# Sums taken on VectorE in halves before two chains of TensorE products, in the edge sort of a graph layer

## The chip, the cores and the metric

The kernel runs on one core of a Trainium2 chip. Its time is the device time of one execution in microseconds (us). TensorE is called PE in the profile, VectorE is DVE, ScalarE is ACT, GpSimd is POOL, and SyncE is SP.

## The reference

There are 8192 nodes with 512 features, and 131072 edges (src, dst, weight), sorted by dst.

```python
h   = layernorm(x) @ gnn_weight.T
msg = edge_weight[:, None] * h[dst]
x   = x + segment_sum(msg, src, 8192)      # added up by src
x   = x + ffn(layernorm(x))                # seven layers of width 160 on two positions of a row,
                                           # their inputs and the output of 32 columns are one-hot nibbles
```

The edges are sorted by dst, but the sum is over src. So the kernel must first bring the edges into the order of their src block (64 blocks of 128 nodes), and then gather rows of h by dst.

## The kernel before

**Projection** (`project`, lines 176 to 245): a loop over the 64 blocks of 128 rows. VectorE takes the statistics of a pair of blocks, ScalarE scales it, TensorE turns a block (L213, four transposes) and multiplies it with the weights (L238), ScalarE evicts, and SP writes h_rows to memory. The statistics and scaled rows are issued four blocks ahead.

**The sort** (`order`, L537) is done in two parts, of 7 and 9 chunks. Each part goes through its chunks (`chunk`, L328) and then a squeeze (`squeeze`, L410), which closes the gaps in the placed cells. A chunk holds 64 edges in each of 128 partitions, as 8 columns c of 8 groups g. It does this:

- VectorE builds `hot`, the one-hot of the src block of each edge (128 x 8 x 64 x 8, bf16; L334).
- TensorE adds up, over the partitions above and all columns, how many edges of each block there are: `p_base`, eight accumulating products with the matrix `above` (L342). ScalarE copies it to `cum[:, 0]` (L344).
- VectorE forms running sums over the columns in `cum` (L347) and masks them with `hot` (L351). Each edge has one block, so in a masked column only one of 64 values counts.
- TensorE sums these: eight products with the identity add eighths of the 64 blocks into `p_rank` (L357), and VectorE reduces the last eight (L361).
- VectorE turns a rank into a slot (`at`, L376) and two value tiles (`put`, L384); ScalarE copies `hot` to f32 as `blocks` (L375); TensorE places the edges with many small products, `p_c` (L402), in four bursts, each of which the trace shows as 64 matrix instructions.

The tiles `hot`, `cum` and the others of a chunk have one buffer each; `put` and `blocks` have two.

**The order of work.** PE, DVE, ACT and SP issue in the order of the program text, which a planner with generators writes. `chunk` and `squeeze` yield a pair (tiles, blocks): how many gather tiles, or projection blocks, are to be issued before the next step. A zero means that the next step follows at once.

The first part runs beside the projection, and only `blocks` counts: a chunk takes six blocks, and base and rank are issued two blocks apart, with `fine` off, so that an operation is not cut. Once the first part ends, up to BEGUN steps of the second part are issued in the projection's last blocks, and then the steps up to number BEGUN + 16:

```python
while first is None and begun < BEGUN and due <= b + 1:
    due += next(second)[1]
    begun += 1
...
for n in range(BEGUN + 16):
    if n >= begun:
        next(second)
```

The rest of the second part runs beside the first gathers (`begin`, L874), with `fine` on, so that an operation is cut into pieces. There `tiles` counts, multiplied with PACE (the first value for chunks, the second for the squeeze):

```python
while t >= due:
    due += next(second, (NB * FT,))[0]
```

**Gathers.** GpSimd fetches rows of h by index (`rows_for`, L570, one indirect DMA per tile of 128 edges, four tiles per buffer, six buffers). For a tile, VectorE builds a weighted one-hot (L583), issued 28 tiles ahead, and TensorE multiplies it with the rows (L870, two instructions per tile in the trace, and one small `p_j` product per buffer, L866). VectorE adds a finished block to x (L880). The first part has 6 tiles per block, 384 in all (`begin`); the second 11, 704 in all (`evenly`, L903), with the network (`ffn`, L693) beside them. The second part's gathers need the second squeeze, which is issued to its end by tile 355.

Of the kernel before, what the change touches and what calls it, by code (L numbers as in the profile page):

```python
# [9 lines left out]
BF16 = mybir.dt.bfloat16  # L10
# [3 lines left out]
OP = mybir.AluOpType  # L14
# [20 lines left out]
def tile_gnn_ffn(  # L35
# [23 lines left out]
    nc = tc.nc  # L59
    P = 128  # L60
    N, D = x.shape
    E = src.shape[0]
    NB = N // P
# [7 lines left out]
    GC, GQ, CAP, SUB = 8, 8, 40, 2  # L71
# [13 lines left out]
    GS = 4  # L85


    SHARE, TURN, WIDTH, PACE = 0.5, 0.6, 640, (1.0, 0.85)
    assert E % P == 0 and D == 512 and NB == 64 and N <= 1 << DSTS and LOW + BITS <= 31
    assert N % (P * U) == 0 and GB * NG == P and all(NB * n % GS == 0 for n in TILES)  # L90

# [173 lines left out]
    above = ec.tile([P, P], BF16, name="above")  # L265
# [57 lines left out]
    def cut(n, size, fine):  # L323

        parts = -(-n // size) if fine else 1
        return [slice(n * i // parts, n * (i + 1) // parts) for i in range(parts)]

    def chunk(ck, ps_c, q, col, fine):  # L328


        hot = ck.tile([P, GC, NB, GQ], BF16, name="hot")
        for cs in cut(GC, 2, fine):
            n = cs.stop - cs.start
            nc.vector.tensor_tensor(  # L334
                hot[:, cs], each.rearrange("p (o b) g -> p o b g", o=1).to_broadcast([P, n, NB, GQ]),
                blk[:, q, cs].rearrange("p c (o g) -> p c o g", o=1).to_broadcast([P, n, NB, GQ]),
                OP.is_equal)
            yield 1, cs.stop // GC

        p_base = ps_c.tile([P, NB, GQ], F32, name="p_base")  # L340
        for c in range(GC):
            nc.tensor.matmul(p_base, above, hot[:, c], start=(c == 0), stop=(c == GC - 1))  # L342
        cum = ck.tile([P, GC, NB, GQ], BF16, name="cum")
        nc.scalar.copy(cum[:, 0], p_base)  # L344
        yield 2, 0
        for c in range(1, GC):
            nc.vector.tensor_tensor(cum[:, c], cum[:, c - 1], hot[:, c - 1], OP.add)  # L347
            if c % 2:
                yield 1, 0
        for cs in cut(GC, 2, fine):  # L350
            nc.vector.tensor_tensor(cum[:, cs], cum[:, cs], hot[:, cs], OP.mult)  # L351
            yield 1, 0
        yield 0, 2
        p_rank = ps_c.tile([P, GC, NB // GC, GQ], F32, name="p_rank")
        nb = NB // GC
        for i in range(GC):
            nc.tensor.matmul(p_rank, eye, cum[:, :, i * nb : (i + 1) * nb, :], start=(i == 0),  # L357
                             stop=(i == GC - 1))
        yield 2, 0
        rank = ck.tile([P, GC, GQ], F32, name="rank")  # L360
        nc.vector.tensor_reduce(rank, p_rank.rearrange("p c b g -> p c g b"), AX.X, OP.add)  # L361
        slot = ck.tile([P, CG, 1], BF16, name="slot")
        nc.vector.tensor_tensor(slot[:, :, 0], rank.rearrange("p c g -> p (c g)"), par, OP.add)
        yield 1, 0
        at = ck.tile([P, CG, 2, HALF], BF16, name="at")
        ready = {}

        def prepare(c0):

            if c0 >= GC:  # L370
                return
            n = SUB * GQ
            cs = slice(c0 * GQ, c0 * GQ + n)
            blocks = ck.tile([P, SUB, GQ, NB], F32, name="blocks", bufs=2)
            nc.scalar.copy(blocks, hot[:, c0 : c0 + SUB].rearrange("p c b g -> p c g b"))  # L375
            nc.vector.tensor_tensor(  # L376
                at[:, cs].rearrange("p n h s -> p n (h s)"),
                lots.rearrange("p (o h) s -> p o (h s)", o=1).to_broadcast([P, n, CAP]),
                slot[:, cs].to_broadcast([P, n, CAP]), OP.is_equal)
            yield 1, 0  # L380
            put = ck.tile([P, n, 2, 2, HALF], F32, name="put", bufs=2)
            for i, val in enumerate((val_a, val_w)):
                v = val[:, q, c0 : c0 + SUB, :].rearrange("p c (g a b) -> p (c g) a b", a=1, b=1)
                nc.vector.tensor_tensor(put[:, :, :, i, :], at[:, cs],  # L384
                                        v.to_broadcast([P, n, 2, HALF]), OP.mult)
                yield 1, 0
            ready[c0] = blocks, put

        yield from prepare(0)
        yield 0, 1  # L390
        yield from prepare(SUB)
        p_c = ps_c.tile([P, GQ, 2, HALF], F32, name="p_c")
        yield 0, 1
        nc.tensor.matmul(p_c.rearrange("p g w s -> p (g w s)"), nil[:, :P], nil, start=True,
                         stop=False)
        for c0 in range(0, GC, SUB):
            blocks, put = ready.pop(c0)
            for k in range(SUB * GQ):
                c, g = divmod(k, GQ)
                last = c0 + SUB == GC and k == SUB * GQ - 1  # L400
                for h in range(2):
                    nc.tensor.matmul(p_c[h * NB : (h + 1) * NB, g], blocks[:, c, g, :], put[:, k, h],  # L402
                                     start=False, stop=last)
            yield from prepare(c0 + 2 * SUB)
            yield 1, c0 // SUB % 2 if c0 + SUB < GC else 0
        for i, cells in enumerate((cells_a, cells_w)):
            nc.scalar.copy(cells[:, col : col + GQ * HALF].rearrange("p (g s) -> p g s", s=HALF),
                           p_c[:, :, i, :])
# [128 lines left out]
    def order(part):  # L537

        qs, col, fine = (range(QA), 0, 0) if part == 0 else (range(QA, NQ), CARRY, 1)
        with tc.tile_pool(name="ck", bufs=1) as ck, \  # L540
                tc.tile_pool(name="ps_c", bufs=1, space=PSUM) as ps_c:
            for q in qs:
                for tiles, blocks in chunk(ck, ps_c, q, col, fine):
                    yield tiles * PACE[0], blocks
                col += GQ * HALF
        with tc.tile_pool(name="sq", bufs=1) as sq, \
                tc.tile_pool(name="ps_q", bufs=2, space=PSUM) as ps_q:
            for tiles, blocks in squeeze(part, sq, ps_q, fine):
                yield tiles * PACE[1], blocks
# [42 lines left out]

    LEAD, BEGUN = 2, 24
    due, early, begun = LEAD, 0, 0
    for b, _ in enumerate(heads):
        while first and due <= b + 1:
# [548 lines left out]
```

## Time and profile before

| | us |
|---|---|
| median of 3 runs (2081.74 to 2099.45) | 2087.55 |
| the profiled execution | 2087.88 |
| its span, first to last instruction | 2086.0 |
| PE busy | 1752.6 (84%) |
| DVE busy | 988.5 (47%) |
| ACT busy | 389.3 (19%) |
| POOL busy | 1113.9 (53%) |
| p_base products, L342, x128 | 31.7 busy |
| p_rank products, L357, x128 | 31.8 busy |
| first indirect gather starts at | 369.7 |
| second squeeze starts at | 836.5 |

The busy time of an engine is the union of its instructions, so that eight products that overlap in the pipeline count once. The mean of one product (393 ns) includes the time to its modelled end; the time from one start to the next is what a product takes from the others. In a line of the timeline the bracket at the end gives the idle time of the engine before the instruction, and what released it. The granted clock of TensorE is given as a share of full speed; its mean over the execution is 0.908.

### The profile page before, as it was taken

What the parts mean: (1) busy time and instruction counts of PE and PEld (TensorE: products, weight loads), DVE (VectorE), ACT (ScalarE), POOL (GpSimd) and SP (SyncE); (2) the same over time, 40 slices, a digit from 0 to 9 for tenths busy, and PEclk for the clock granted to TensorE, in tenths of its full rate; (3) what the DMA queues carried; (4) which work ended last, traced back from release to release, by engine and by line L of the source; (5) the groups of instructions that cost most, each with busy time, mean ns of one, the idle gap of its engine ahead of it and who ended that gap; (6) DMA issues with size and microseconds to landing.
All of it is one profiled execution on the core that took longest, in us unless ns stands there. A gap on an engine that the chain in (4) does not pass through costs nothing.

```text
span 2086.0 us, 24100 instructions
## 1 busy us (share of the span) xinstructions
PE 1752.6 (84%) x9288; PEld 845.7 (41%) x9288; DVE 988.5 (47%) x2520; ACT 389.3 (19%) x521; POOL 1113.9 (53%) x1138
## 2 busy tenths in 40 slices
PE   7999989589889988976877697896978969697977
PEld 4555544344444444322332243342434334243444
DVE  6676787365545554983332334233333334234422
ACT  5565644211201211110000010100101001010111
POOL 4000000466657666787666666666666766666540
PEclk9999999699989998988999899998989979898986
DMA  5233332567667776677876667686676857667651
GB/s 174 82 102 102 102 93 84 150 198 218 209 205 217 220 222 214 191 229 226 259 264 190 174 186 262 181 274 174 191 258 176 275 169 218 217 172 244 198 148 35
DMA packets 140923, 391.37 MB, mean 188 GB/s; under 512 B 20352, under 2 KB 21376, under 8 KB 140800
## 3 DMA queue, kind: packets, MB, share of 16 engines
q0 software_dynamic: 87952, 286.45, 46.0%
q1 hardware_dynamic: 52048, 101.72, 14.4%
q8 instruction: 76, 1.25, 0.2%
q10 hardware_dynamic: 800, 1.57, 0.2%
q14 instruction: 47, 0.39, 0.1%
HBM read 339.33 MB, written 50.33 MB: 187 GB/s over the span
## 4 chain that ended last, share of the span: by engine, by line
PE 65%; issue 10%; DVE 9%; another core or an unknown queue 8%; POOL 6%; DMA 2%; ACT 1%; POOLq 0%; DVEq 0%; ACTq 0%
PE p_g L870 36%; PE p_g L238 8%; PE p_c L402 7%; POOL g L570 6%; PE p_a L666 2%; PE p_a L668 2%; DVE hot L583 2%; PE p_rank L357 1%; PE p_base L342 1%; DMA g<-h_rows,at_dst 1%; PE p_g L213 1%; PE p_j L866 1%; PE p_b L660 1%; DVE ln L706 1%
## 5 line engine op out<-in xcount | busy, mean ns | idle before, releaser
L570 POOL DMA_INDIRECT g<-h_rows,at_dst x1088 | 1091.6, 1003 | 906.7 <-issue 645.2
L870 PE MATMUL p_g<-g,hot 128*128 128x512 f32 x2176 | 1098.9, 640 | 42.1 <-issue 42.0
L870 PEld LDWEIGHTS p_g<-g,hot 128*128 128x128 f32 x2176 | 407.6, 201 | 438.9 <-issue 428.0
L583 DVE TENSOR_SCALAR hot<-lanes,at_row,at_w 128x128 f32<-128x128 f32 x1088 | 325.6, 354 | 235.5 <-remote 143.7
L238 PE MATMUL p_g<-xg,g 128*128 128x512 f32 x512 | 235.8, 604 | 5.1 <-ACT g L215 5.1
L402 PE MATMUL p_c<-put,blocks 128*64 128x40 f32 x4096 | 163.9, 237 | 66.0 <-issue 62.7
L402 PEld LDWEIGHTS p_c<-put,blocks 128*64 128x64 f32 x4096 | 147.6, 146 | 110.0 <-issue 102.4
L375 ACT CAST blocks<-hot 128x1024 f32<-128x1024 bf16 x64 | 131.4, 2078 | 251.4 <-issue 213.8
L238 PEld LDWEIGHTS p_g<-xg,g 128*128 128x128 f32 x512 | 94.1, 194 | 101.3 <-issue 94.4
L640 DVE TENSOR_SCALAR hb<-p_b,b_b 128x128 f32<-128x128 f32 (+1 forms) x54 | 18.1, 335 | 244.5 <-PE p_b L660 84.8
L866 PEld LDWEIGHTS <-hot 128*1 128x1 bf16 x272 | 21.5, 79 | 241.0 <-issue 208.2
L384 DVE TENSOR_TENSOR put<-at,val_a 128x640 f32<-128x640 bf16 x64 | 52.7, 824 | 110.4 <-remote 57.9
L866 PE MATMUL p_j<-g,hot 128*1 128x4 bf16 x272 | 45.7, 168 | 54.1 <-DMA g<-h_rows,at_dst 29.5
L347 DVE TENSOR_TENSOR cum<-cum,hot 128x512 bf16<-128x512 bf16 x112 | 47.8, 427 | 88.9 <-ACT cum L344 73.3
L643 ACT ACTIVATE ha<-p_a,b_a 128x512 f32<-128x512 f32 (+1 forms) x54 | 34.5, 640 | 231.9 <-PE p_g L870 94.1
L923 DVE TENSOR_TENSOR xu<-xu,p_g 128x512 f32<-128x512 f32 x64 | 43.5, 680 | 72.1 <-remote 37.6
L880 DVE TENSOR_TENSOR xg<-xg,p_g 128x512 f32<-128x512 f32 x64 | 43.6, 681 | 69.2 <-PE p_g L870 56.0
L760 ACT COPY back<-p_v 128x256 f32<-128x256 f32 (+1 forms) x9 | 3.3, 371 | 383.0 <-PE p_v L758 166.0
L171 ACT ACTIVATE rstd_f<-mv_f,eps 128x8 f32<-128x8 f32 (+1 forms) x9 | 2.7, 300 | 384.9 <-issue 200.5
L668 PEld LDWEIGHTS p_a<-hb,w_z 128*128 128x128 f32 x360 | 52.7, 211 | 18.4 <-issue 17.3
L213 PE MATMUL p_g<-ident,g 128*128 128x128 f32 x256 | 40.3, 282 | 18.0 <-ACT g L204 12.9
L717 PE MATMUL p_v<-mask,before 128*128 128x8 f32 (+1 forms) x18 | 4.8, 340 | 57.3 <-DVE both L714 27.2
(180 smaller groups left out, 1199.6 us busy)
## 6 DMA issues: line engine op xcount, KB each, us to landing
g<-h_rows,at_dst POOLq DMA_INDIRECT x1088
xg<-in_x_dram SPq DMA_DIRECT2D x16, 1024.0 KB
x_rows<-xg SPq DMA_DIRECT2D x32, 512.0 KB
xu<-x_rows SPq DMA_DIRECT2D x16, 1024.0 KB
g<-in_x_dram SPq DMA_DIRECT2D x31, 512.0 KB
h_rows<-g SPq DMA_DIRECT2D x31, 512.0 KB
out_dram<-xu SPq DMA_DIRECT2D x7, 2048.0 KB
xg<-in_gnn_wT_dram ACTq DMA_DIRECT2D x1, 1024.0 KB
```

The costliest lines, as they stand in the source:

```text
L213: nc.tensor.transpose(p_t[:, k * P : (k + 1) * P], t[:, 2 + b % 2, k * P : (k + 1) * P], ident)
L238: nc.tensor.matmul(p_h, t[:, b % 2, k * P : (k + 1) * P], gw[:, k, :], start=(k == 0), stop=(k == KD - 1))
L347: nc.vector.tensor_tensor(cum[:, c], cum[:, c - 1], hot[:, c - 1], OP.add)
L375: nc.scalar.copy(blocks, hot[:, c0 : c0 + SUB].rearrange("p c b g -> p c g b"))
L384: nc.vector.tensor_tensor(put[:, :, :, i, :], at[:, cs], v.to_broadcast([P, n, 2, HALF]), OP.mult)
L402: nc.tensor.matmul(p_c[h * NB : (h + 1) * NB, g], blocks[:, c, g, :], put[:, k, h], start=False, stop=last)
L570: nc.gpsimd.indirect_dma_start(out=g[:, k, :], out_offset=None, in_=h_rows, in_offset=bass.IndirectOffsetOnAxis(ap=at_dst[part][:, i : i + ...
L583: nc.vector.tensor_scalar(hots[n][:, k, :], lanes, at_row[part][:, i : i + 1], at_w[part][:, i : i + 1], op0=OP.is_equal, op1=OP.mult)
L668: nc.tensor.matmul(p_a[:, g, :], w_z[:, i, g, :], last_hb, start=False, stop=((g + 1) * T % 512 == 0 or g == NG - 1))
L866: nc.tensor.matmul(p_j[:, part, :], hot[:, GS - 1, :].bitcast(BF16)[:, 1:2], g.rearrange("p k d -> p (k d)").bitcast(BF16).rearrange("p (k ...
L870: nc.tensor.matmul(p_g, hot[:, i, :], g[:, i, :], start=(k == 0), stop=(k == TILES[part] - 1))
L880: nc.vector.tensor_add(xg[:, b % G, :], xg[:, b % G, :], p_g)
```

## The change

Three things change in `chunk`. Ahead of base, VectorE adds the eight columns of `hot` pairwise until two are left: three adds of two columns each, the sums held in the last two columns of `cum`, which is not yet in use. `p_base` then takes two products instead of eight. After the masking, VectorE adds the upper half of the 64 blocks to the lower half, and again with 32, so that 16 are left; `p_rank` takes two products instead of eight. The results are whole numbers that bf16 holds, so they stay the same.

The new steps yield (1, 0): in the first part they follow at once, in the second they are one paced tile apart. A chunk of the second part has 39 paced tiles instead of 33, and the first value of PACE goes from 1.0 to 0.84. BEGUN goes from 24 to 30.

```diff
-    SHARE, TURN, WIDTH, PACE = 0.5, 0.6, 640, (1.0, 0.85)
+    SHARE, TURN, WIDTH, PACE = 0.5, 0.6, 640, (0.84, 0.85)
...
+        cum = ck.tile([P, GC, NB, GQ], BF16, name="cum")
+        two = cum[:, GC - 2 :]
+        for c in range(2, GC, 2):
+            nc.vector.tensor_tensor(two, hot[:, 0:2] if c == 2 else two, hot[:, c : c + 2], OP.add)
+            yield 1, 0
         p_base = ps_c.tile([P, NB, GQ], F32, name="p_base")
-        for c in range(GC):
-            nc.tensor.matmul(p_base, above, hot[:, c], start=(c == 0), stop=(c == GC - 1))
-        cum = ck.tile([P, GC, NB, GQ], BF16, name="cum")
+        for c in range(2):
+            nc.tensor.matmul(p_base, above, two[:, c], start=(c == 0), stop=(c == 1))
...
         for cs in cut(GC, 2, fine):
             nc.vector.tensor_tensor(cum[:, cs], cum[:, cs], hot[:, cs], OP.mult)
             yield 1, 0
+
+        for nb in (NB // 2, NB // 4):
+            for cs in cut(GC, GC // 2, fine and nb == NB // 2):
+                nc.vector.tensor_tensor(cum[:, cs, :nb], cum[:, cs, :nb], cum[:, cs, nb : 2 * nb],
+                                        OP.add)
+                yield 1, 0
         yield 0, 2
...
-        for i in range(GC):
+        for i in range(2):
             nc.tensor.matmul(p_rank, eye, cum[:, :, i * nb : (i + 1) * nb, :], start=(i == 0),
-                             stop=(i == GC - 1))
+                             stop=(i == 1))
...
-    LEAD, BEGUN = 2, 24
+    LEAD, BEGUN = 2, 30
```

## The prediction

> **What bounds the kernel now.** I read the utilisation by slice first, then a table of stages, then the order of time inside one chunk of each stage, and last the waits.
>
> ```profile
> PE   7999989589889988976877697896978969697977
> ...
> DVE  6676787365545554983332334233333334234422
> ```
>
> The stages (columns: stretch, length, busy us of each engine, granted clock, DMA share, GB/s):
>
> ```profile
> core 0: us, PE busy (x) PEld busy (x) DVE busy (x) ACT busy (x) POOL busy (x), PEclk, DMA share, GB/s
> ...
> 20.00:270.00 250.00, 250.00 (x2436) 147.18 (x2434) 165.71 (x291) 148.32 (x204) 5.66 (x11) 1.00 0.31 97
> 270.00:345.00 75.00, 64.76 (x190) 30.12 (x190) 68.70 (x110) 37.95 (x63) 0.00 (x0) 0.95 0.31 98
> ...
> 410.00:836.00 426.00, 379.13 (x2757) 193.62 (x2755) 232.73 (x536) 76.78 (x64) 274.50 (x256) 0.92 0.69 209
> 836.00:966.00 130.00, 103.46 (x228) 41.47 (x226) 111.85 (x249) 15.11 (x13) 101.88 (x80) 0.88 0.72 221
> ```
>
> Chunks 1 to 7 run from 20 to 270 us, beside the projection: TensorE (PE) is busy all the time, VectorE (DVE) 66%. The first squeeze (270 to 345) keeps VectorE at 92%. Chunk 8 straddles the change to the gathers; chunks 9 to 16 run from 407 to 836, PE 89%, VectorE 55%. Then comes the second squeeze, and from 966 gathers and network, which do nothing of the change and merely start earlier or later. So TensorE time removed from the chunks shortens the run, as long as VectorE does not become late for it. The squeezes move as blocks.
>
> One early chunk, in order of time (start, duration):
>
> ```profile
> 95.08 0.16 DVE L202 SCALAR_TENSOR_TENSOR nmr_h<-mv_h,rstd_h 128x2 f32<-128x2 f32 x1
> ...
> 97.30 1.89 PE L342 MATMUL p_base<-hot,above 128*128 128x512 bf16 x8
> ...
> 99.23 0.58 ACT L344 CAST cum<-p_base 128x512 bf16<-128x512 f32 x1 [1.14 <-PE p_base L342]
> ...
> 99.84 3.18 DVE L347 TENSOR_TENSOR cum<-cum,hot 128x512 bf16<-128x512 bf16 x7 [4.61 <-ACT cum L344]
> ...
> 103.06 2.29 DVE L351 TENSOR_TENSOR cum<-cum,hot 128x4096 bf16<-128x4096 bf16 x1
> ...
> 106.77 1.89 PE L357 MATMUL p_rank<-cum,eye 128*128 128x512 bf16 x8
> ```
>
> The reader is to see that base and rank each hold TensorE without a gap, and that VectorE ends the masked sums (105.35) only 1.4 us before rank starts: that is its whole slack.
>
> **What goes.** TensorE loses 12 of 16 products per chunk. The next transposes start at 99.03, so eight cost 1.73 us, 0.215 each; 12 are **2.58 us per chunk**.
>
> **What comes.** Three adds of 128x1024 bf16 on the one-hot columns, then one of 2048 and one of 1024 elements (in late chunks two of 1024 and one of 1024). The masking multiply has this form and type: 0.68 us at 1024, 2.29 at 4096, hence an estimate of 1.22 at 2048. Dependent operations follow each other 0.03 us after an end (seven in 3.18). So 2.1 us ahead of base, 1.9 ahead of rank. The halved views are strided; no row has that. Lower end: as the multiply. Upper end: the rate of the f32 adds, 0.68 us for 512 (L880), so 1.2 for 1024 and 2.3 for 2048. I take the lower: the runs are 256 and 128 elements long and the operation and type are the multiply's.
>
> **Early chunks (7).** In VectorE's queue the adds follow nmr (done 95.24), which waits for ScalarE, which waits for TensorE's transposes at 93.37; they end at 97.35, and base starts 0.1 late. Its last product ends 0.42 after its start; ScalarE copies at 98.10 instead of 99.23; the scan starts at 98.71, masking ends at 104.22, the two folds at 106.18. TensorE arrives at rank 1.2 us earlier than before, at 105.57: **a new stall of 0.65 us**. Behind the folds on VectorE wait the batch statistics of a later block, now 0.85 us later (105.27 to 106.1). Their scaled rows are turned three blocks on, over 11 us later. Behind them come the reduction of rank and the puts: these stay at their old time while TensorE is earlier; the first product that reads a put was at 116.47, its put done at 112.0, so 4.4 us of slack become 2.6. ScalarE's next statistics step waits for the next transposes again, so each chunk begins with the old phase. Net 2.58 - 0.10 - 0.65 = 1.83; seven give **-12.8 us**. Without this cover (VectorE a further 1.83 late) they would give nothing.
>
> **Chunk 8 (347 to 407).** Four one-hot builds for the gather stage stand ahead of the adds in VectorE's queue, ending at 350.92; base waits till 353.05 instead of 351.06 (+2.0 - 1.3), rank till 362.0, and TensorE passes it 0.2 late. [...] I count 0.
>
> **Chunk 9.** BEGUN and the steps issued ahead now end with the second add, so base and its scan come two tiles into the gather stage. Before:
>
> ```profile
> 407.32 3.39 PE L342 MATMUL p_base<-hot,above 128*128 128x512 bf16 x8
> ...
> 420.49 3.50 PE L357 MATMUL p_rank<-cum,eye 128*128 128x512 bf16 x8 [2.32 <-DVE cum L351]
> ```
>
> Both at half the clock. From 407.32 to 423.92 are 16.6 us, with eight tiles of 0.93: 9.1 us for the two products and a stall. After: 0.43 each, 0.5 stall, and the low clock falls on two tiles (+1.8), about 3.2 to 4. **-5 us** (between 0 and -7).
>
> **Chunks 10 to 16 (7).**
>
> ```profile
> 459.38 1.89 PE L342 MATMUL p_base<-hot,above 128*128 128x512 bf16 x8
> ...
> 461.93 0.42 DVE L347 TENSOR_TENSOR cum<-cum,hot 128x512 bf16<-128x512 bf16 x1 [2.51 <-issue]
> ...
> 468.98 0.68 DVE L351 TENSOR_TENSOR cum<-cum,hot 128x1024 bf16<-128x1024 bf16 x1
> ...
> 470.58 1.89 PE L357 MATMUL p_rank<-cum,eye 128*128 128x512 bf16 x8
> ```
>
> A chunk has 33 paced tiles before, 39 x 0.84 = 32.8 after, so the squeeze begins at the same tile and no load, store or gather (all tied to tiles) passes another queue. Inside the chunk tiles move. Base to rank: TensorE had 1.73 + 10 tiles; it gets 0.43 + 13 x 0.84 = 10.9 tiles of 0.93, 10.7 us with gaps. VectorE: scan start 2.54 - 1.29 = 1.25 us after base; scan and mask 7.7 as now (it holds eight one-hot builds and one accumulation between); three folds at a pitch of 0.60, one more one-hot and a share of an accumulation, 2.2: 11.2 in all. **Stall 0.5 us** (0 to 1.5), where 0.9 us were left. Ahead of base the adds (2.6 with one-hots between) get 1.9 tiles more, 1.75 us, beside 2 to 6 us of slack: nothing. The tiles come from between the bursts of p_c, where TensorE starves:
>
> ```profile
> 590.17 0.34 PE L402 MATMUL p_c<-put,blocks 128*64 128x40 f32 x5 [0.36 <-issue]
> 590.90 0.36 PE L402 MATMUL p_c<-put,blocks 128*64 128x40 f32 x5 [0.39 <-issue]
> ```
>
> [...] If that region (25 to 31 us; 17.3 with no gap and the full clock) is bound so, its length hardly shrinks when 1.6 of its 10 tiles go, and these cost up to 1.5 us elsewhere; if not, nothing. No row tells; I take 0.6. Net 2.58 - 0.5 - 0.6 = 1.5; **-10 us** (between -18 and 0).
>
> Gathers keep up: they wait for TensorE to free buffers, 58.1 us in 430 to 800. [...] All 3.9 us of late adds turned into delay would be under the 8 us per chunk that GpSimd waits for TensorE: still hidden.
>
> **Sum.** 12.8 + 0 + 5 + 10 = 28 us. The profiled execution took 2087.9 us (span 2086.0); that becomes 2060. It equals the median of 2087.55 within 0.4 us, so **2060** for the median too.
>
> **Rivals.**
> (1) *The late gain is eaten.* The starved p_c regions are the limit, tiles moved out of them cost 1.5 us, and chunk 9 stays as it was: 2.58 - 0.5 - 1.5 = 0.6 per late chunk, 4 in all. With the early 12.8: 2071. For it: TensorE idles nearly only in p_c in that stage (41.7 us). Against: in five of seven such regions at least one burst of 64 runs without a gap.
> (2) *VectorE takes over and the clock falls.* The strided folds cost the upper end: +1.6 us in each chunk. Rank stalls 2.3 early, 2.1 to 2.6 late. This trace drops the clock after gaps of 2.32 (above: 3.50 for 1.89) and 2.33, not after 1.97: +1.7 us. Early: 0.1 + 2.3 + 1.7 - 2.58 = +1.5, times 7 is +11; late +1.7, times 8 is +14: 2112. It decides from a fold of about 1.2 us per 1024. [...]
> (3) *No change:* VectorE simply late everywhere, stalls of about 2.5 us per chunk without the clock: 2087. The waits speak against it: VectorE idles 4.61 us before each early scan, which the earlier base gives back.
>
> **How the numbers follow.** Forecast 0.62, (1) 0.20, (2) 0.08, (3) 0.10. The forecast's own range is 2048 to 2070: early gain 8 to 16, late 4 to 23. With (1) whole and part of (3): 2045 to 2084. A measurement tells 1%, 21 us, from no change. Faster: nearly all of the forecast, little of (1): 0.61. Same: most of (1), all of (3): 0.31. Slower: 0.08.
>
> **What would show it.** Right: base and rank as x2 of about 0.6 us; a wait of rank for the folds of 0.4 to 0.9 us; the folds 0.68 and 1.22 us; the first gather at 357 instead of 369.7; the second squeeze at 808 instead of 836; the clock at 1.00 from 20 to 250. Wrong: folds near 1.2 per 1024, rank waiting over 2 us with long matmuls after it, or p_c regions longer than their 25 to 31 us.

## The result, and the profile after

The changed kernel took **2106.22 us** (median of 14 runs, 2094.07 to 2115.71) against 2089.62 us for the kernel before, run beside it (14 runs): ratio 1.0073, 95% interval 1.0055 to 1.0091. The forecast was 2060, so it missed by 46 us and its sign was wrong; the range of 2045 to 2084 does not hold the result. Its size is within 1% of no change. The profiled execution took 2104.1 us, with a span of 2102.3 against 2086.0. Of the signs that the prediction named, the first gather came at 378.0 us (357 forecast, 369.7 before), the second squeeze at 845.7 (808 forecast, 836.5 before), and the granted clock from 20 to 270 us fell to 0.98.

The utilisation by slice of the changed kernel:

```profile
PE   6999998587888888874887598896978969697976
...
DVE  7777778466565656983232234242342334234422
```

TensorE is less busy in the first slices and VectorE more, as an exchange of work should look. TensorE's share falls in the middle too, but the span grew. The stages of the changed kernel (columns as in the table of before):

```profile
20.00:270.00 250.00, 233.21 (x2207) 134.34 (x2208) 190.48 (x324) 145.27 (x199) 5.80 (x12) 0.98 0.30 95
270.00:345.00 75.00, 65.99 (x305) 32.06 (x303) 64.69 (x96) 36.03 (x60) 0.00 (x0) 0.95 0.31 99
...
410.00:836.00 426.00, 361.74 (x2610) 187.29 (x2610) 253.57 (x562) 74.97 (x65) 282.69 (x252) 0.89 0.66 205
836.00:966.00 130.00, 100.63 (x332) 41.90 (x331) 106.45 (x232) 17.23 (x14) 98.49 (x77) 0.89 0.71 219
```

In the 250 us of the early chunks TensorE was busy all the time before; now it is idle for 17 us, and has done less by 270 us: x2207 products for x2436. Only 84 of the products that are missing are those of the change (12 in each of seven chunks); the others were pushed past 270, and the next stretch has x305 for x190. So the freed time did not shorten the stage; it became waiting. From 410 to 836 TensorE is less busy too: 361.74 us for 379.13.

Where the 16 us arise can be read from the starts of the base products in the two profiles (one of each). The seventh chunk starts 7.7 us late (244.41 for 236.69), the first gather comes 8.3 late, the ninth chunk starts 11.9 late (419.17 for 407.32), the tenth 14.5 (473.83 for 459.38), the sixteenth 15.8 (800.23 for 784.45), and the last gather is 15.8 late too. Half of the loss is early, most of the rest lies in chunks 8 and 9, and behind the chunks nothing is added.

What TensorE waits for from 20 to 345 us, in the changed kernel (total, times, longest):

```profile
PE p_g L238 <- ACT g L215: 17.6, 12, 1.8
PE p_rank L368 <- DVE cum L361: 4.3, 7, 0.6
PE p_g L213 <- ACT g L240: 4.2, 3, 1.8
```

The second line is the stall that was forecast, 0.61 us in each of seven chunks. The first was not: projection products wait for ScalarE's eviction of the turned block, 12 times, 17.6 us (before: 5 times, 5.1 us, all in the squeeze); seven of the twelve are one in each chunk, of 1.77 us. In the order of time of one early chunk, these instructions stood so before the change:

```profile
107.06 0.30 ACT L195 ACTIVATE rstd_h<-mv_h,eps 128x2 f32<-128x2 f32 x1 [2.88 <-DVE mv_h L193]
...
109.67 2.06 ACT L375 CAST blocks<-hot 128x1024 f32<-128x1024 bf16 x1
...
111.63 0.58 ACT L215 COPY g<-p_g 128x512 f32<-128x512 f32 x1
...
112.81 3.60 PE L238 MATMUL p_g<-xg,g 128*128 128x512 f32 x8
```

and so after it:

```profile
105.12 1.95 DVE L361 TENSOR_TENSOR cum<-cum 128x2048 bf16<-128x2048 bf16 x2
106.99 0.69 DVE L192 BATCH_NORM_STATS2 st_h<-g 128x6 f32<-128x512 f32 x1
107.12 0.59 PE L368 MATMUL p_rank<-cum,eye 128*128 128x512 bf16 x2 [0.61 <-DVE cum L361]
107.55 0.60 PE L213 MATMUL p_g<-ident,g 128*128 128x128 f32 x4
...
108.78 0.29 ACT L195 ACTIVATE rstd_h<-mv_h,eps 128x2 f32<-128x2 f32 x1 [5.03 <-DVE mv_h L193]
...
109.50 1.52 ACT L204 ACTIVATE g<-g,nmr_h,rstd_h 128x512 f32<-128x512 f32 x2 [0.43 <-DVE nmr_h L202]
...
110.93 0.56 ACT L240 COPY g<-p_g 128x512 f32<-128x512 f32 x1
...
111.39 2.04 ACT L386 CAST blocks<-hot 128x1024 f32<-128x1024 bf16 x1
...
113.34 0.57 ACT L215 COPY g<-p_g 128x512 f32<-128x512 f32 x1
...
113.97 5.40 PE L238 MATMUL p_g<-xg,g 128*128 128x512 f32 x8 [1.77 <-ACT g L215]
```

Read the second one upwards. L238 waits for L215, the eviction of the block that TensorE turned at 107.55 (`turn` runs one block ahead of the multiply). Its data are ready at 108, but L215 stands in ScalarE's queue behind the cast of `blocks` (2.04 us), this behind an eviction and the scaling L204, and that behind L195, which waits for the statistics L192. These stand behind the two folds in VectorE's queue. ScalarE sat idle for 5.03 us ahead of all of it. The folds reach TensorE a second time, by way of ScalarE. The sum comes out: before, L215 was done 0.6 us ahead of L238 (112.21 for 112.81). Counted from base, the change brings TensorE to L238 1.5 us sooner (14.0 us for 15.5) and ends L215 0.8 us later (15.7 for 14.9); 1.5 and 0.8 less the 0.6 are the wait of 1.77 within 0.1.

The last line took 5.40 us where the same eight products took 3.60 in the trace of before: the granted clock is 1.00 up to 114 us and 0.50 from 116 to 118.

From base to base an early chunk took 34.85 us before. It takes 35.29 in four chunks after and 36.98 in the three in which the clock falls (by the records of the granted clock for 3.4 us each time, which at half speed is 1.7 us lost). Summed, 4 x 0.44 + 3 x 2.13 = 8.2 us; the first gather starts at 378.0 instead of 369.7, which is that sum within 0.1.

In the gather stage the bursts of p_c have stretches like this one, in the changed kernel:

```profile
503.92 0.22 PE L413 MATMUL p_c<-put,blocks 128*64 128x40 f32 x1 [0.45 <-issue]
504.63 0.32 PE L413 MATMUL p_c<-put,blocks 128*64 128x40 f32 x1 [0.48 <-issue]
506.72 0.23 PE L413 MATMUL p_c<-put,blocks 128*64 128x40 f32 x1 [1.77 <-issue]
507.42 0.23 PE L413 MATMUL p_c<-put,blocks 128*64 128x40 f32 x1 [0.47 <-issue]
```

One pair per 0.7 to 2.1 us, with no releaser that the trace knows. This is the worst stretch, and such ones stand in the trace of before as well. The gaps did not grow longer (0.56 us on average in chunks 9 to 16, as before), but there were more of them, 102 for 71. Between 410 and 836 us they came to 58.3 us, 39.7 before; since some of chunk 8's gaps moved into that stretch, the sum over the whole execution is the better measure: 78.7 for 62.7.

### The profile page after: what moved, and what is told of

It reads as the page before. It is cut to its first block, busy times and chain, and to the rows that moved or that the text cites. A ratio compares the mean times of both kernels' runs of the same rounds, so it can differ in the third digit from the quotient of the medians.

```text
span 2102.3 us, 23823 instructions
## 1 busy us (share of the span) xinstructions
PE 1720.8 (82%) x9096; PEld 829.3 (39%) x9096; DVE 1049.5 (50%) x2609; ACT 388.4 (18%) x521; POOL 1128.5 (54%) x1138
## 4 chain that ended last, share of the span: by engine, by line
PE 57%; DVE 17%; another core or an unknown queue 11%; issue 9%; ACT 3%; POOL 2%; DMA 1%; DVEq 0%; ACTq 0%; POOLq 0%
PE p_g L881 35%; PE p_c L413 8%; PE p_g L238 4%; DVE hot L594 3%; PE p_a L677 2%; PE p_a L679 2%; DVE cum L352 2%; POOL g L581 2%; DVE cum L356 2%; DVE cum L361 1%; DMA g<-h_rows,at_dst 1%; DVE st_h L192 1%; PE p_j L877 1%; PE p_a L663 1%
## 5 line engine op out<-in xcount | busy, mean ns | idle before, releaser
L581 POOL DMA_INDIRECT g<-h_rows,at_dst x1088 | 1106.2, 1017 | 907.7 <-issue 651.3
L881 PE MATMUL p_g<-g,hot 128*128 128x512 f32 x2176 | 1094.0, 638 | 38.9 <-issue 38.1
L238 PE MATMUL p_g<-xg,g 128*128 128x512 f32 x512 | 240.6, 614 | 18.0 <-ACT g L215 18.0
L413 PE MATMUL p_c<-put,blocks 128*64 128x40 f32 x4096 | 170.5, 237 | 82.0 <-issue 78.7
L238 PEld LDWEIGHTS p_g<-xg,g 128*128 128x128 f32 x512 | 95.4, 196 | 118.7 <-issue 97.1
L213 PE MATMUL p_g<-ident,g 128*128 128x128 f32 x256 | 40.8, 284 | 18.1 <-ACT g L204 12.8
L387 DVE TENSOR_TENSOR at<-lots,slot 128x640 bf16<-128x640 bf16 x64 | 52.4, 819 | 0.3
```

The source lines that it names most:

```text
L238: nc.tensor.matmul(p_h, t[:, b % 2, k * P : (k + 1) * P], gw[:, k, :], start=(k == 0), stop=(k == KD - 1))
L387: nc.vector.tensor_tensor(at[:, cs].rearrange("p n h s -> p n (h s)"), lots.rearrange("p (o h) s -> p o (h s)", o=1).to_broadcast([P, n, C ...
L581: nc.gpsimd.indirect_dma_start(out=g[:, k, :], out_offset=None, in_=h_rows, in_offset=bass.IndirectOffsetOnAxis(ap=at_dst[part][:, i : i + ...
L881: nc.tensor.matmul(p_g, hot[:, i, :], g[:, i, :], start=(k == 0), stop=(k == TILES[part] - 1))
```

## The experiments

The runs went to five chips in five groups, each beside the kernel before, whose median there was 2091.0, 2115.5, 2091.3, 2111.5 and 1855.0 us. The fifth is spoken of at the end. "p_c gaps" are the gaps without a releaser on p_c in the whole profiled execution (62.7 us before, 78.7 in the changed kernel); one profile of each, so only large differences count, and they do not stand for the time: e2 and e4 are slower than before with gaps hardly larger or smaller, e3 is faster with larger ones. Ratios from different groups come from different chips, which is itself a difference.

| run | what it is | ratio to before | interval | p_c gaps |
|---|---|---|---|---|
| e1_pace_alone | before, with the change's empty steps, PACE 0.84, BEGUN 30 | 1.0013 | 0.9992 to 1.0033 | 63.3 |
| e2_old_pace | whole change, no tiles, PACE 1, BEGUN 30 | 1.0060 | 1.0036 to 1.0084 | 57.9 |
| e3_base_alone | adds and short base, no tiles, PACE 1, BEGUN 27 | 0.9976 | 0.9959 to 0.9993 | 76.0 |
| e4_rank_alone | folds and short rank, no tiles, PACE 1, BEGUN 27 | 1.0063 | 1.0039 to 1.0086 | 63.6 |
| e5_late_only | whole change and settings, last nine chunks only | 1.0035 | 1.0015 to 1.0055 | 85.6 |
| e6_early_base | adds and short base, first seven chunks only | 0.9959 | 0.9940 to 0.9979 | 65.5 |
| e7_pool_cast | change in the first seven chunks, one cast on GpSimd | 0.9962 | 0.9944 to 0.9979 | 56.6 |
| e8_spread | before, six tiles moved to the bursts of p_c | 0.9972 | 0.9948 to 0.9996 | 53.9 |
| e9_adds_unread | before, with the late adds, unread | 1.0004 | 0.9983 to 1.0026 | 65.4 |
| e10_late_free | change late only, no tiles, PACE 1, BEGUN 24 | 0.9956 | 0.9937 to 0.9975 | 63.7 |
| e11_more_products | before, 12 products more per late chunk | 1.0022 | 1.0007 to 1.0037 | 39.0 |
| e12_both | e6 and e8 together | 0.9925 | 0.9900 to 0.9950 | 60.2 |
| e13_free_24 | whole change, no tiles, PACE 1, BEGUN 24 | 0.9965 | 0.9947 to 0.9983 | 62.0 |
| e14_tiles_24 | as e5, but BEGUN 24 | 1.0061 | 1.0039 to 1.0084 | 92.5 |
| e15_before_18 | before, BEGUN 18 | 0.9965 | 0.9938 to 0.9991 | 62.9 |
| e16_free_30 | as e10, but BEGUN 30 | 0.9954 | 0.9925 to 0.9983 | 69.8 |
| e17_all (fifth chip) | short base everywhere, short rank late, no tiles | 0.9996 | 0.9988 to 1.0005 | 0 |
| e18_all_spread (fifth chip) | e17 with e8's tiles | 0.9989 | 0.9982 to 0.9996 | 0 |

**The planner's settings without the work**, and **the work without the settings.** e1 adds only empty steps:

```diff
+        for c in range(2, GC, 2):
+            yield 1, 0
...
+        for c in range(3 if fine else 2):
+            yield 1, 0
```

> The kernel before with only the six empty paced steps, PACE 0.84 and BEGUN 30: no add, eight products each. Theory A (two causes: early, ScalarE's queue behind the folds; late, the bursts of p_c take as long as their instructions need to arrive, so tiles moved out from between them are paid again elsewhere): early unchanged, first gather at 370 us; late, the p_c regions stay at 27 to 29 us though 1.6 tiles shorter, and base to rank grows by about one tile: +1.5 to +2.5 us per late chunk, 12 to 20 us in all, about 2104. Theory B (VectorE is simply late for the products, pacing costs nothing): within 4 us of 2088.

e2 is the changed kernel with `yield 0, 0` for the new steps and PACE (1.0, 0.85).

> The whole change, but its new steps are worth no tile and PACE is 1.0, so that the tiles lie as before the change. A: early as slow as after (first gather 378, +8 us); late, rank waits about 1.1 us for the folds, the p_c regions keep their four tiles between bursts and about 27.6 us, so a late chunk gains about 1.3 us on before, -10 in all: about 2086, some 17 under the changed kernel. B: rank's waits double with fewer tiles before it: 2106 or more.

e1 measured 2096.76 us, 3 over before with an interval that holds zero; e2 2105.86, about 13 over. So the settings alone cost little, and the change loses without them too. Both had been expected otherwise by theory A. Taken alone, this pair pointed away from the pace; later runs put it into another light.

**Base or rank.** e3 leaves out the folds, e4 the adds:

```diff
-        for nb in (NB // 2, NB // 4):
-            for cs in cut(GC, GC // 2, fine and nb == NB // 2):
-                nc.vector.tensor_tensor(cum[:, cs, :nb], ..., OP.add)
...
+        for i in range(GC):
             nc.tensor.matmul(p_rank, eye, cum[:, :, i * nb : (i + 1) * nb, :], ...
```

> Only the adds ahead of base and its two products, no folds, rank with eight; the new steps worth no tile, PACE 1.0. A: nothing stands ahead of the batch statistics in VectorE's queue after the scan, and the scan starts 1.1 us earlier, so ScalarE keeps up with TensorE: early chunk -1.2 us, first gather at 361 or 362; late -1.2 per chunk: about 2070. B: the adds make base wait: 2088 or more.

> Only the folds and rank's two products, base with eight; the new steps worth no tile, PACE 1.0. A: rank waits 0.6 us for the folds, the batch statistics come 2 us later, and the product of the next block waits about 2 us for ScalarE's eviction behind the scaling and the cast: an early chunk is +1 to +2 us, first gather at 378 to 383; late about 0: about 2097. B (only rank's direct wait counts): early -0.7 per chunk, first gather at 365, about 2082.

With base alone an early chunk took 33.59 us, 1.26 less than before, and the first gather started at 361.6, 8.1 us earlier. With rank alone it took 36.4 or 38.1, and the first gather started at 388.4, 18.7 later. So the early loss belongs to the folds. In total e3 gained only 5 us where theory A had 20: part of the early gain was lost again behind the first gather. The projection's products waited for L215 12 times, 16.3 us, in e4.

**The early base by itself, and the early change with ScalarE's queue relieved.** e6 adds up the columns only where `fine` is off and leaves everything else as before. e7 has both parts of the change there, and takes the first cast of `blocks` out of ScalarE's queue:

```diff
+            cast = nc.gpsimd.tensor_copy if c0 == 0 and not fine else nc.scalar.copy
+            cast(blocks, hot[:, c0 : c0 + SUB].rearrange("p c b g -> p c g b"))
```

> Only the adds ahead of base and its two products, and only in the first part; everything else as before. If the early gain passes through the late stage: 1.26 us in each of seven chunks, first gather at 361, total 9 us under before. If the late stage takes it back: first gather at 361, total as before.

> The whole change in the first part only, the late chunks as before; and in the first part the first cast of hot in each chunk goes from ScalarE to GpSimd, which is idle there. Theory A (the cast and the scaling ahead of the eviction in ScalarE's queue make TensorE wait 1.8 us per chunk): that wait is gone, rank still waits 0.6 us, the clock stays up, an early chunk takes 33.0 us instead of 34.85, first gather at 357, total 13 us under before, unless GpSimd takes over 5 us for the cast. Rival (the statistics behind the folds are late for TensorE themselves): the wait stays, first gather at 378.

e6 measured 2105.55 us against 2115.52, ratio 0.9959: faster than the kernel before. e7 gave 0.9962, and its second chunk shows the cause taken away:

```profile
76.76 0.56 ACT L240 COPY g<-p_g 128x512 f32<-128x512 f32 x1
77.22 0.58 ACT L215 COPY g<-p_g 128x512 f32<-128x512 f32 x1
77.37 0.42 PEld L213 LDWEIGHTS p_g<-ident,g 128*128 128x128 f32 x4 [0.79 <-ACT g L240]
77.38 0.66 PE L213 MATMUL p_g<-ident,g 128*128 128x128 f32 x4
77.70 0.59 ACT L240 COPY g<-p_g 128x512 f32<-128x512 f32 x1
77.85 0.30 PEld L238 LDWEIGHTS p_g<-xg,g 128*128 128x128 f32 x2
77.87 3.69 PE L238 MATMUL p_g<-xg,g 128*128 128x512 f32 x8
78.18 2.07 ACT L392 CAST blocks<-hot 128x1024 f32<-128x1024 bf16 x1
```

No cast stands ahead of L215 any more, L238 starts without a wait and runs at the full clock. From rank to the first instruction of p_c it is 8.44 us instead of 10.39 (or 12.08), while the 8.95 from base to rank and the 0.61 of waiting at rank are those of the changed kernel. The chunk takes 33.33 us: 1.52 less than before, where 1.83 had been forecast. **This is the early cause, shown.** The whole gained 8 us and not the 13 expected, because the first chunk missed its gain:

```profile
25.66 2.24 DVE L202 SCALAR_TENSOR_TENSOR nmr_h<-mv_h,rstd_h 128x2 f32<-128x2 f32 x1
25.85 2.02 POOL L392 CAST blocks<-hot 128x1024 f32<-128x1024 bf16 x1
...
30.01 0.64 PE L351 MATMUL p_base<-cum,above 128*128 128x512 bf16 x2 [2.01 <-DVE cum L345]
```

There VectorE's L202, otherwise 0.16 us, took 2.24 beside the cast that the experiment itself had put on GpSimd, and ended with it; the adds behind it came late, base waited 2.01 us and the clock fell again (0.96 from 20 to 60 us). From the second chunk on each gained its 1.5 us. The seventh base came 6.0 us earlier (230.68 for 236.69) and the first gather 5.8 earlier (363.9), so the gathers follow in full.

**The late chunks: which part?** e5 applies the change and its settings only where `fine` is on.

> The change in the chunks of the second part alone (adds, folds, two products each, PACE 0.84, BEGUN 30); the first part as before. Theory C (the late chunks are paced by GpSimd's gathers: the bursts of p_c crawl until the gathers pause, so that TensorE time removed elsewhere comes back as crawl; the added VectorE operations even lengthen the gathers): first gather at 370, mean gather 1.06 us before to 1.10 or more, total 0 to 8 us over before. Theory D (the late chunks gain 1.5 us each as forecast, and one profile only showed it badly): 10 us under before.

It measured 2123.23 against 2115.52, ratio 1.0035. So this version of the late change loses by itself, about 7 us, with an early part that is that of before (first gather 369.9).

e9 keeps all products and adds only VectorE's work, whose sums nothing reads:

```diff
+        if fine:
+            two = cum[:, GC - 2 :]
+            for c in range(2, GC, 2):
+                nc.vector.tensor_tensor(two, hot[:, 0:2] if c == 2 else two, hot[:, c : c + 2], OP.add)
+                yield 0, 0
...
+            for half in (NB // 2, NB // 4):
+                for cs in cut(GC, GC // 2, half == NB // 2):
+                    nc.vector.tensor_tensor(cum[:, cs, :half], ..., OP.add)    # behind rank's products
```

e10 has the same operations, read, and the 12 products fewer, with no tiles and the old settings. e11 instead issues 12 products twice (six of base, as here, and six of rank likewise):

```diff
-        for c in range(GC):
+        for n in (GC - 2, GC) if fine else (GC,):
+            for c in range(n):
-            nc.tensor.matmul(p_base, above, hot[:, c], start=(c == 0), stop=(c == GC - 1))
+                nc.tensor.matmul(p_base, above, hot[:, c], start=(c == 0), stop=(c == n - 1))
```

> The kernel before, with the change's VectorE operations added in the last nine chunks only (three adds of two columns ahead of base, three halvings of cum behind rank's products, no planner tile for them); nothing reads their sums, and base and rank keep their eight products. So TensorE's work is that of before and VectorE has 4.1 us more in each of these chunks. Theory X (VectorE's adds are free there and what counts is TensorE): no change, ratio within 0.002 of 1. Theory Y (the adds slow the gathers that run beside them; the first 280 gathers took 1.114 us each in the changed kernel, 1.064 before): slower by 7 to 28 us, the gathers' mean at 1.09 or more, and the first 280 gathers last over 5 us longer than in a kernel without the adds.

> The whole change in the last nine chunks only, with none of its steps worth a planner tile and the old pace; the first part is that of before. It has the VectorE operations of the run with unread sums and 12 products fewer in each of these chunks, so the difference between the two is what the 12 products are worth there. Theory X (TensorE's time counts, 2.58 us a chunk as predicted): 8 x 2.58 = 20 us under the run with unread sums. Theory Z (TensorE has slack in this stage and the freed time comes back as gaps in the bursts of p_c): within 5 us of the run with unread sums, gaps without a releaser on p_c of 45 us or more between 410 and 836 us, against 39.7 before. If the planner's tiles made the late loss of the late-only run (7 us), this one is within 3 us of before.

> The kernel before with 12 products more in each of the last nine chunks: six of base and six of rank are issued twice, the first time into sums that the second overwrites. TensorE's work there goes up by what the change takes off, and no other engine's changes. If TensorE's time sets this stage (the prediction's step, 2.58 us a chunk): slower by 8 x 2.58 = 20 us, ratio 1.0095. If TensorE has slack there: slower by less than 7 us, with smaller gaps on p_c or shorter waits elsewhere.

Measured on one chip: e9 1.0004, e10 0.9956, e11 1.0022. VectorE's adds by themselves cost nothing that these runs can tell (-4 to +5 us). Taking 12 products away gains the difference of e9 and e10, 10 us; putting 12 on costs 4.6. By TensorE's time both would be 8 x 2.58 = 20.6. But in e10, with no tiles beside the folds, rank waits for them, 11.2 us in seven chunks, which e9 has not; what is left of the 20.6 is near the 10 gained. So taking away shows no discount on TensorE's time, and only putting on does: a quarter of it reached the total. The groups of p_c, of before and of e11, show where the extra products went (busy, mean ns, then idle before it and by what):

```profile
L402 PE MATMUL p_c<-put,blocks 128*64 128x40 f32 x4096 | 163.9, 237 | 66.0 <-issue 62.7 <-DVE put L384 3.1
```

```profile
L404 PE MATMUL p_c<-put,blocks 128*64 128x40 f32 x4096 | 158.5, 235 | 42.4 <-issue 39.0 <-DVE put L386 2.7
```

With 20.6 us more products, the gaps of p_c shrank by 23.7. The gaps give way: TensorE's work elsewhere in the chunk seems to fill time that p_c would otherwise lose. With fewer products they did not grow (e10 63.7).

**Tiles or BEGUN.** e5 lost, e10 gained; they differ in the planner's settings alone. e14 is e5 with BEGUN 24, e16 is e10 with BEGUN 30, e13 is e2 with BEGUN 24, and e15 is before with BEGUN 18:

```diff
-    LEAD, BEGUN = 2, 30
+    LEAD, BEGUN = 2, 24
```

> The change in the last nine chunks only, with its tiles and the new pace as in the late-only run (7 us over before), but BEGUN at 24. Theory B: the late gain of 9 less 3 for tiles and pace, 6 us under before, ratio 0.997. Theory P: as the late-only run, 7 us over, 1.0035.

> The change in the last nine chunks only, no tiles, old pace (the run that was 9 us under before), but BEGUN at 30, so that the gathers begin at the same point of the program as in the changed kernel. Theory B: 14 us more than with BEGUN 24, so 5 us over before, ratio 1.0022. Theory P: as with BEGUN 24, 9 us under, 0.9956.

> The whole change with its new steps worth no planner tile, the old pace and BEGUN at the old 24 (the second run of this study, 12.5 us over before, had BEGUN 30). Theory B (six more steps of the second order issued ahead of the gathers cost the late stage its gain): early loss of 8 us and late gain of 9, together within 4 us of before. Theory P (the tiles and the pace are what costs; BEGUN is free): as the run with BEGUN 30, 12 us over before, ratio 1.006. Theory N (the early and the late part disturb each other): also 12 over.

> The kernel before with BEGUN 18 for 24, nothing else: six steps of chunk 9 fewer are issued ahead of the gathers. If the point of the program at which the gathers begin is what gave the free late-only run its gain: under before by 5 to 14 us. If it is the 12 products: within 3 us of before.

e14 1.0061 and e16 0.9954: theory P. For the late-only change **the tiles and the pace are what costs, and BEGUN shows no effect**: 1.0035 and 1.0061 with them, 0.9956 and 0.9954 without, whichever BEGUN. The means differ by 0.93%, some 19 us; e14 and e16, on one chip, by 22. The gaps of p_c go the same way, here in e14 and then in e16:

```profile
L418 PE MATMUL p_c<-put,blocks 128*64 128x40 f32 x4096 | 172.7, 237 | 96.3 <-issue 92.5 <-DVE put L400 3.4
```

```profile
L418 PE MATMUL p_c<-put,blocks 128*64 128x40 f32 x4096 | 166.5, 238 | 72.9 <-issue 69.8 <-DVE put L400 2.7
```

22.7 us more gaps, with the same instructions on every engine (these two profiled executions differ by 9 us only). What the settings do there: of the 32.8 tiles of a chunk more go between the adds and the folds, and 8.4 instead of 10 between the steps of p_c.

A rival stands beside the gaps: TensorE's granted clock. Its mean over the runs behind each ratio is 0.898 in e5 and in e14, 0.905 in e16 and 0.909 in e10; 0.909 in e1, where the same tiles go with all products and cost 3 us; 0.902 in the changed kernel; and 0.906 to 0.910 in the kernel before, on the four chips that these runs had. The 0.007 between e14 and e16 are an estimated 15 us at full speed, of the 22 that they differ by. Whether the gaps bring the clock down or only come with it, no run separates.

e13 measured 0.9965, 7 us under before. It has the changed kernel's instructions and differs from it only in tiles, PACE and BEGUN: 1.0073 against 0.9965, some 22 us. But e2, with BEGUN 30 and no tiles either, had 1.0060, as slow as the changed kernel. So in the whole change BEGUN seems to matter, which it does not in the late-only one, and the tiles are not shown to be its cost; and e15 shows 7 us for BEGUN in the kernel before (interval 2 to 13). That is not explained by theory B or P, and **stays open**: e2 ran on another chip than e13, with six runs. So does e1, where the same tiles cost only 3 us, on another chip again.

**The other direction.** If tiles taken from the bursts cost time, tiles given to them should gain. e8 does this to the kernel before; e12 adds the early base:

```diff
-            yield 1, cs.stop // GC
+            yield 0, cs.stop // GC
...
-        yield 2, 0                     # behind rank's products
+        yield 0, 0
...
-            yield 1, c0 // SUB % 2 if c0 + SUB < GC else 0
+            yield 1 if c0 < GC // 2 else 4, c0 // SUB % 2 if c0 + SUB < GC else 0
```

> The kernel before with six of a late chunk's 33 tiles moved: none between the one-hot builds, none after rank, and four instead of one after the third and fourth burst of p_c. No instruction is added or taken. If the crawl is a matter of a store of instructions that is refilled between bursts: gaps in p_c fall from 40 to below 25 us in 410 to 836, total 10 to 20 us under before. If the crawl simply lasts until the gathers pause: gaps and total as before, within 5 us.

> Two edits together that each alone was under the kernel before: base from two products in the first part only (9 to 10 us under) and the six planner tiles moved from between the steps of hot and rank to the bursts of p_c (4 to 6 us under). They act in different stages, so the sum is expected: 14 us under, ratio 0.9935, first gather at 362 us, gaps without a releaser on p_c between 410 and 836 us at 30 us. If the gain of one is only the other's (both merely start the gathers in another phase), no more than 9 under, ratio 0.996.

e8 gave 0.9972, 6 us where 10 to 20 had been expected, with gaps of 29.2 us on p_c between 410 and 836 (39.7 before), not under 25. e12 gave 2075.78 against 2091.33 in six runs, **0.9925, the best ratio of all**, and the sum of the two gains as expected (its gaps there were 36.7 us, 30 expected). It keeps the part of the change that paid and has no folds.

**The sum of what paid.** e17 takes base from two products everywhere and rank from two only late, without tiles; e18 adds e8's tiles.

> What the runs so far leave of the change: base from two products in every chunk, rank from two products in the last nine chunks only, no planner tile for the new steps, old pace, BEGUN 24. The early part is that of the early-base run (9 us under before), the late part that of the free late-only runs (9 to 10 under). If the two parts add up: 18 us under before, ratio 0.9915, first gather at 362 us. If they take from each other, as the whole change did: no better than the better of the two, 0.9955.

> The same with the six planner tiles moved from between the steps of hot and rank to the later bursts of p_c (alone 6 us under before, and with the early base 16 under). If the bursts of p_c still gain by more gathers between them: 24 us under before, ratio 0.9885. If the freed TensorE time and the moved tiles fill the same gaps: as the run without the move, 0.9915. With six tiles fewer around rank the folds have less cover: a wait of rank for the folds of over 2 us in each late chunk, and then slower than the run without the move.

They came to a chip on which the kernel before took 1855.03 us, and there neither moved the time by more than 0.1%. The kernel before was not profiled there; its mean granted clock was 0.963, for 0.906 to 0.910 on the others. The group of the gathers, in the trace of before, from a slower chip, and in e17 (idle before them, and by what):

```profile
L570 POOL DMA_INDIRECT g<-h_rows,at_dst x1088 | 1091.6, 1003 | 906.7 <-issue 645.2 <-PE p_g L870 150.2 <-remote 93.8
```

```profile
L586 POOL DMA_INDIRECT g<-h_rows,at_dst x1088 | 1105.7, 1016 | 669.9 <-issue 626.5 <-DMA g<-h_rows,at_dst 30.8 <-PE p_g L886 8.3
```

and the bursts of e17:

```profile
L418 PE MATMUL p_c<-put,blocks 128*64 128x40 f32 x4096 | 132.9, 232 | 3.7 <-DVE put L400 3.3 <-ACT blocks L391 0.4
```

No gap of p_c without a releaser is left, and GpSimd hardly waits for TensorE (8.3 us for 150.2). Through the late chunks GpSimd issues gathers without a pause of over 1 us, so that it seems to set the pace itself; in the trace of before such pauses take 92 us of the first 280 gathers. That would make TensorE's time in the late chunks worth nothing there. It does not explain the early part: e17's first gather came at 361.0, as expected, and a queue that never pauses should have carried this to the end. That VectorE's added operations make the gathers longer there (1016 ns on average for the 1003 of the trace of before) is a rival that no run on that chip tests. Whether the gains add up on a chip of the slower kind stays untested.

## Why the prediction was wrong

**Early chunks, -12.8 forecast, +8.3 measured.** The direct terms were right: base's two products took 0.59 us and started 0.05 late (0.1 forecast), the stall at rank was 0.61 (0.65), the folds 1.95 together (1.9), and the way from base to rank became 0.53 shorter (0.65 by the working). The step that failed is this one: the statistics behind the folds come 0.85 late, but "their scaled rows are turned three blocks on, over 11 us later", and "ScalarE's next statistics step waits for the next transposes again, so each chunk begins with the old phase". It followed the data of the late instruction to its reader. It did not ask what is queued behind it on ScalarE: an eviction, a cast of 2.06 us and the eviction L215, which had 0.6 us of slack in the trace of before and was asked for 1.5 us sooner. In its place came a wait of 1.77 us in each of the seven chunks. e7 shows it: with one cast out of that queue the chunk takes 33.33 us. What is left to the forecast, 0.31 a chunk, was not sought.

The clock added to it. In three of seven chunks it halved after waits of 0.61 and 1.77 us, 6.8 us apart, neither of which reaches the 2.32 us on which the prediction set its bound. It took single gaps one by one, and its own trace had a case against that: two waits of 1.79 and 1.67 us beside the first squeeze, which end at 285.95 and 288.28, with the granted clock at 0.50 from 288 to 292. The three halvings cost 3 x 1.69 = 5.1 us of the early chunks' time. Why three of the seven chunks are hit and four are not, with the same two waits in each, no run shows.

**Late chunks, -15 forecast, about +8 in the changed kernel's profile, +7 and +13 where they change alone.** Chunk 8 was counted as 0 and chunk 9 as -5; together they cost some 6 us (8.3 late at the first gather, 14.5 at the tenth base), though chunk 9 lost its stall of 2.32 us and the low clock behind it, as forecast. No run shows the 0: from its base to the next, chunk 8 took 58.05 us after and 56.26 before. From the tenth base to the sixteenth nothing came of the -1.5 a chunk; it was +1.3 in all.

The term that failed is that of the moved tiles. The prediction saw that 1.6 tiles leave the bursts of p_c and took 0.6 us a chunk, with 1.5 in its first rival; in the late-only change e5, e10, e14 and e16 give 19 / 8 = 2.4. It had named the sign that it would be wrong by, "p_c regions longer than their 25 to 31 us": they went from 27.8 to 28.6 on average, with fewer tiles in them. The working held the 32.8 tiles of a chunk for the same as 33; that was right for the squeeze and no answer for where in the chunk they lie. A second term was put at nothing: the sum has no change of the granted clock behind chunk 9, and by its records TensorE was at half clock for 89 us between the ninth base and the end of the chunks, 74 before. How much of the tiles' cost is the clock, and why e2 loses as much with no tiles, stays open. The stall at rank was right (0.5 forecast, 3.8 us in seven chunks). That the products' 2.58 us were counted too high is not shown: e11 says so, e9 and e10 do not.

**Right for the wrong reason, and right.** The second rival ended at 2112, near the result, but by folds at twice their time and stalls at rank of over 2 us, neither of which came: luck. That VectorE's added operations would not hold the gathers up measurably was right (e9: ratio 1.0004, with 1007 ns a gather for the 1003 of before). The first rival had the late mechanism in part and kept the early gain, which was lost too.

## What to carry to other kernels

When work is put ahead of an instruction in one in-order queue, follow every engine that waits for that instruction and what stands behind it in that engine's own queue, not only the reader of its data; here an eviction behind a 2 us cast had 0.6 us of slack, came 0.8 us later and was needed 1.5 us sooner, and the engine that sets the end waited for it in every chunk. Where a planner's pace is changed along with the work, run the two apart (here the same instructions were 0.4% faster than the kernel before under the old settings, e13, and 0.7% slower under the new ones, each on its own chip). Where TensorE's time changes in a stage with gaps that have no releaser, look at these gaps and at the granted clock too: in e11 three quarters of what was added never reached the total, while the gaps shrank.

## What the runs showed of the hardware

Two short waits a few microseconds apart, 0.61 and 1.77 us, were followed by half the clock in three of seven equal chunks: 5.40 us for eight products that take 3.60, with 3.4 us at half clock each time. In the kernel before, waits of 1.79 and 1.67 us were too, with the granted clock at 0.50 from 288 to 292 us.

The bursts of p_c, 64 small products each, starve without a releaser while the gathers run and never in the early chunks: the first such gap ends at 371.76 us in the kernel before and at 381.46 in the changed one, the first gather starts at 369.7 and 378.0. In chunks 9 to 16 there were 71 such gaps in the kernel before and 102 in the changed one, of 0.6 us on average in both. On one of five chips the runs e17 and e18 have no such gap, and the kernel before takes 1855.0 us there instead of 2091.0 to 2115.5 on the other four. What TensorE waits for in these gaps, no view of the traces shows.
